# A mamba and spectral-filter kernel: other order of the first loads, later constants, and a second block whose first tiles lie under tiles that are dead in the last chunk

## The chip, the cores and the metric

The kernel runs on one core of a Trainium2 chip. The metric is the device time of one execution in microseconds (us), the median of several runs. A core has five engines with a queue of instructions each: TensorE (PE, matmuls), VectorE (DVE), ScalarE (ACT), GpSimd (POOL) and SyncE (SP, which here only issues transfers). They meet through semaphores: an instruction that isn't ready holds all that stand behind it on its engine. Transfers (DMAs) run on 16 DMA engines that all queues share.

## The reference

Two layers in float32 on x of shape (4, 128, 128, 128): 4 images of 128 channels, with 128 x 128 = 16384 pixels that the first layer takes as a sequence.

```python
# layer 0, per image; l runs over 16384 pixels
h1 = relu(xf @ mlp_w1.T + mlp_b1);  xm = h1 @ mlp_w2.T + mlp_b2
x_in, z = split(xm @ in_proj_w.T)                 # 256 channels each
u = silu(causal_conv4(x_in) + conv_b)
dt, Bm, Cm = split(u @ x_proj_w.T)                # 8, 16, 16
delta = softplus(dt @ dt_proj_w.T + dt_proj_b)
h = h * exp(delta * A) + delta * B * u            # a scan over l, 256 x 16 states
y = sum_s(h * C) + u * D
out = (y * silu(z)) @ out_proj_w.T                # 128 channels
x1 = silu(group_norm(out, 4)) + x
# layer 1
a = relu(agg_w @ group_norm(concat(x1, x1), 32) + agg_b)
weights = softmax(mean(a) @ wg_w.T + wg_b)        # 4 per image
xf = rfft2(x1)
ff = rfft2(irfft2(xf * filter_f))                 # f = 0..3
result = irfft2(sum_f weights_f * xf * ff_f) + residual_weight * x1
```

## The kernel before, in words

**Block 0** takes the sequence of each image in 32 chunks of 512 pixels, so 128 chunks in all, k = 0 to 127. A chunk has 8 units (two halves j of the 256 channels, four groups r of four states), each of two pairs, so NP = 16 slots per chunk. A table `todo[slot, phase]` holds functions; a loop runs over the slots and, in each, over the phases ("turn", "sums", "pe", "exps", "late", "act", "pool", "dbu", "early", "gate", "scans", "dve", "end"), and calls them. This order, written by hand, is the order in which each engine's queue is filled (`tc.manual_schedule()`). `pre(k)` lists a chunk's preparation with slots counted from the chunk before: load of x, the small matrix products, the convolution (`cv_mm` into two of the "pp" banks of PSUM, `silu_act` out of them), x_proj (`xd_mm`, `xd_act`), dt (`dt_act` makes delta), and the product delta x u (`du_pool`, on POOL, L319).

The scan needs each channel's row on the partitions of several states. So delta, du, B and C are written to DRAM (dd, bc) and read back, repeated over partitions: `bc_load` reads rB and rC (L270, four transfers each), `rep_load(j)` reads rdelta and rdu (L327, four each). All are issued by SP, in order. A transfer that reads dd or bc waits for the store to have landed.

In a unit, ACT makes da = exp(delta A) (L400), POOL makes hb = rdu x rB for three of four states (L370, `dbu`), PE turns bt into b0 for the fourth (L390), DVE scans (L419) and multiplies two of the scans by rC (L421), POOL multiplies the others (L426), and PE sums over states (L440). PSUM has one bank each for b0, da1, da2 and da3, so ACT can't be far ahead of DVE.

`first_constants` loads what a chunk needs. `later_constants`, called in phase "end" of slot 4, loads out_wT (wo) and 15 constants of the norms and of block 1 on SP, then lets DVE negate fwm (L129) and set eps and ones (L131, L133). `later_products`, slot 8, has DVE make weff0 (L138, L139) and bias0 (L144), the latter from two matmuls of PE into a "pp" bank (L143).

From slot 26 on of each chunk, `post(k)` gates y with silu(z), multiplies by wo, takes sums for the norm (L463, L464) and stores o to DRAM (L465, on SP). The norms, the `agg` step of block 1 and some forward spectra of finished images run in the same slots, for images 0 to 2.

**Block 1** works in units of 8 channels of one image (64 units), three sub-blocks each: forward transform on PE (over_h, over_w; L873, L892; or a spectrum that block 0 stored, sx), the mix of the four filters by the image's weights (`term` on ACT L840, `mix` on POOL L850 or DVE L848), the products on DVE, the inverse transform, the residual (L949) and the store. The norm of image 3 runs among the first units. A filter tile ft has four transfers (L819) of 8 channels for one of the four filters each. SP loads, in order: the three constants c_ihc, c_ihs, c_iw (L764), xt1 and sx of the first unit, xt1 of the second, ft_0, and so on.

Tiles come from pools. A pool's memory is laid out once, and block 1's pools start at the address at which block 0's did, so that its tiles lie over block 0's. The first transfer into such a tile waits until the last reader or writer of what lies under it is done. Before, `late` and the big tiles of block 1 lie over p1 and p2 of block 0, which hold, among much else, small tiles that the softmax of image 2 uses to the end of block 0.

```python
        todo[4, "end"].append(partial(s.later_constants, s))
        todo[8, "end"].append(partial(s.later_products, s, psum))
```

Of the kernel before, what the change touches and what calls it, by code (L numbers as in the profile page):

```python
# [46 lines left out]
def kernel(ctx: ExitStack, tc: tile.TileContext, a: dict, out: bass.AP):  # L47
# [32 lines left out]
    def first_constants(s):  # L80
# [26 lines left out]
        for j in range(NH):  # L107
            nc.vector.tensor_scalar_mul(s.diag[:, j, :], s.ident, dvec[:, j : j + 1])

    def later_constants(s):  # L110
        s.wo = const("wo", [P, NH, C], a["out_wT"].rearrange("(j p) c -> p j c", p=P))
# [16 lines left out]
        s.fwm = const("fwm", [W, 2 * WF], a["c_fwi"])  # L128
        nc.vector.tensor_scalar_mul(s.fwm, s.fwm, -1.0)  # L129
        s.eps = cpool.tile([P, 1], F32, tag="eps", name="eps")  # L130
        nc.vector.memset(s.eps, EPS)  # L131
        s.ones = cpool.tile([P, P], F32, tag="ones", name="ones")
        nc.vector.memset(s.ones, 1.0)  # L133

    def later_products(s, psum):

        weff0 = s.weff0 = cpool.tile([P, C], F32, tag="weff0", name="weff0")
        nc.vector.tensor_scalar_mul(weff0, s.wagg[:, 0, :], s.gam[:, 0:1])  # L138
        nc.vector.scalar_tensor_tensor(weff0, s.wagg[:, 1, :], s.gam[:, 1:2], weff0, ALU.mult, ALU.add)  # L139
# [20 lines left out]
def block0(tc, s):  # L160
# [4 lines left out]
    with ExitStack() as ctx:  # L165
        def pool(name, bufs, **kw):
            return ctx.enter_context(tc.tile_pool(name=name, bufs=bufs, **kw))

        p1 = pool("p1", 1)
        p2 = pool("p2", 2)  # L170
        hpool = pool("hb", 4)
        tiny = pool("tiny", 2)
        dbc = pool("dbc", 2, space=DRAM)
        s.own, s.spare = p1, p2
        psp = pool("psp", 2, space=PSUM)
# [13 lines left out]
        def pre(k):  # L189
# [7 lines left out]
            def load():  # L197
                xt = d["xt"] = p1.tile([P, T], F32, tag="xt", name=f"xt_{k}")
                (nc.sync if k else nc.scalar).dma_start(out=xt, in_=s.xflat[b, :, i * T : (i + 1) * T])
# [6 lines left out]
            def h1_act():  # L206
                d["h1"] = p1.tile([P, NH, T], F32, tag="hd", name=f"h1_{k}")
                for j in range(NH):
                    nc.scalar.activation(d["h1"][:, j, :], ps["h", j], AF.Relu, bias=s.b1[:, j : j + 1])
# [47 lines left out]
            def xd_act():  # L257
                xd = d["xd"] = p1.tile([P, TH], F32, tag="xd", name=f"xd_{k}")
# [6 lines left out]
            def bc_load():  # L265
                for q, tag in enumerate("BC"):
                    t = d[tag] = p2.tile([P, NG - 1 + q, T], F32, tag=f"r{tag}", name=f"r{tag}_{k}")
                    rows = d["bc"][q, (1 - q) * SQ :, :].rearrange("(g s) t -> s g t", s=SQ)
                    for m in range(SQ):
                        nc.sync.dma_start(out=t[m * DG : (m + 1) * DG], in_=rows[m].partition_broadcast(DG))  # L270
# [8 lines left out]
            def dt_act():  # L279
                delta = d["delta"] = p1.tile([P, NH, T], F32, tag="hd", name=f"delta_{k}")  # L280
# [11 lines left out]
            def xd_turn_act():  # L292
                d["xdt"] = p1.tile([P, NT, NX], F32, tag="xdt", name=f"xdt_{k}")
                src = ps["xt"][:, 0:2, :].rearrange("p t (h r) -> p h t r", h=2)
                nc.scalar.copy(d["xdt"].rearrange("p (h t) r -> p h t r", h=2), src[:, :, :, 0:NX])
# [10 lines left out]
            def bt_act(h, n0, n1):  # L306

                if h == n0 == 0:
                    d["bt"] = p2.tile([P, NT, NH * ND, SQ, DG], F32, tag="bt", name=f"bt_{k}")
                for n in range(n0, n1):  # L310
# [6 lines left out]
            def du_pool():  # L317
                du = d["du"] = p1.tile([P, NH, T], F32, tag="du", name=f"du_{k}")
# [3 lines left out]
            def rep_load(j):  # L322
                for q, tag in enumerate(("delta", "du")):
                    t = d[tag, j] = p2.tile([P, ND, T], F32, tag=f"r{tag}", name=f"r{tag}_{k}_{j}")
                    rows = d["dd"][q, j * P : (j + 1) * P, :].rearrange("(g d) t -> d g t", d=DG)
                    for m in range(SQ):
                        nc.sync.dma_start(out=t[m * DG : (m + 1) * DG], in_=rows)  # L327
# [116 lines left out]
        def post(k):  # L444
# [12 lines left out]
            def o_act():  # L457
# [6 lines left out]
                nc.scalar.activation(d["po"], d["po"], AF.Square, accum_out=stats[b][:, 1, i : i + 1])  # L464
                nc.sync.dma_start(out=outs[b][:, i * T : (i + 1) * T], in_=d["o"])  # L465

# [271 lines left out]
def block1(tc, s):  # L738
# [10 lines left out]
    with ExitStack() as ctx:  # L749
        def pool(name, bufs, **kw):  # L750
            return ctx.enter_context(tc.tile_pool(name=name, bufs=bufs, **kw))

        late = pool("late", 1)
        p2 = pool("f2", 2)
        psa = pool("psa", 1, space=PSUM)
        psx = pool("psx", 2, space=PSUM)
# [5 lines left out]
        def const(name, shape):  # L762
            t = late.tile(shape, F32, tag=name, name=name)
            nc.sync.dma_start(out=t, in_=s.a[name])  # L764
            return t
# [32 lines left out]
        N = len(units)  # L798
        u = [SimpleNamespace() for _ in units]

# [15 lines left out]
        def load_filter(ft):  # L816
            ft.t = p2.tile([H, NF, CC, 2 * WF], F32, tag="ft", name=f"ft_{ft.first}", bufs=KEEP)
            for f in range(NF):
                nc.sync.dma_start(out=ft.t[:, f], in_=filt[:, f, ft.c0 : ft.c0 + CC, :])  # L819

        def load(n):
            if n < N:
                c0, b = units[n]
                u[n].xt = p2.tile([H, CC, W], F32, tag="xt1", name=f"xt1_{n}", bufs=6)
                nc.sync.dma_start(out=u[n].xt, in_=s.x1[b][c0 : c0 + CC].rearrange("c h w -> h c w"))
                u[n].early = units[n] in s.spectra
                if u[n].early:
                    u[n].sx = p2.tile([H, CC, 2, WF], F32, tag="sx", name=f"sx_{n}", bufs=2)
                    nc.sync.dma_start(out=u[n].sx, in_=s.spec[b][:, c0 : c0 + CC])
# [242 lines left out]
```

## Time and profile before

| | us |
|---|---|
| median of 3 runs (7092.60 to 7100.89) | 7099.01 |
| the profiled execution's own time | 7100.83 |
| its span, first to last instruction | 7099.1 |
| VectorE busy | 6843.7 |
| GpSimd busy | 6807.6 |
| ScalarE busy | 6144.4 |
| block 0 ends (last o computed) | 6391.7 |
| mean granted TensorE clock | 0.926 |

The profile is one execution. Busy time is the sum of an engine's instructions; a line of a timeline gives the start, the length, the engine, the line of the code, the operation, what it writes and reads, and in square brackets how long the engine had stood idle before it and what ended that. "x4" means four instructions merged into one line. An engine with q behind its name (SPq, ACTq) issues a transfer: the length is that of the issue, and the data moves later. Where an instruction waits for several things, the one that the profile names may not be the last.

### The profile page before, as it was taken

How to read it: one execution, taken by the hardware profiler on the slowest of the kernel's cores; microseconds unless marked ns; L12 is line 12 of the kernel's file. 1: busy time of each engine (PE TensorE's matmuls, PEld its weight loads, DVE VectorE, ACT ScalarE, POOL GpSimd, SP SyncE). 2: the span in 40 equal slices, each digit the busy share in tenths (PEclk: the TensorE clock that was granted, in tenths of full speed). 3: DMA queues.
4: the chain of work that ended last, by engine and by line, in shares of the span. 5: the costliest groups of instructions: out<-in, count | busy, mean ns of one | idle time of the engine just before them, and what ended most of it. 6: DMA issues, size and time to landing. Idle time of an engine off the chain costs nothing.

```text
span 7099.1 us, 95554 instructions
## 1 busy us (share of the span) xinstructions
PE 5656.9 (80%) x28724; PEld 2700.3 (38%) x28724; DVE 6843.7 (96%) x7901; ACT 6144.4 (87%) x13836; POOL 6807.6 (96%) x3010
## 2 busy tenths in 40 slices
PE   6777777787777778787787778887778787877999
PEld 2333333333333333333333333333333333327888
DVE  6999999999999999999999999999999999997877
ACT  6888888888888888888989888898988989878886
POOL 6999999999999999999999999999999999997887
PEclk8988898888989989999999999999999999989999
DMA  6667667667787767777777777777878777768865
GB/s 141 160 153 164 159 149 165 160 150 175 179 196 181 188 169 167 181 181 179 192 193 196 189 174 177 174 184 172 200 188 200 191 170 178 169 143 293 273 218 190
DMA packets 759513, 1288.54 MB, mean 182 GB/s; under 512 B 81728, under 2 KB 192848, under 8 KB 758992
## 3 DMA queue, kind: packets, MB, share of 16 engines
q1 hardware_dynamic: 758848, 1282.16, 72.5%
q8 instruction: 226, 3.70, 0.2%
q14 instruction: 295, 2.42, 0.1%
q10 hardware_dynamic: 144, 0.26, 0.0%
HBM read 1025.52 MB, written 256.58 MB: 181 GB/s over the span
## 4 chain that ended last, share of the span: by engine, by line
ACT 30%; DVE 24%; POOL 18%; PE 10%; issue 10%; DMA 7%; SPq 1%; DVEq 0%; ACTq 0%; POOLq 0%
DVE da L419 12%; ACT da L400 12%; POOL hb L370 10%; POOL hb L426 7%; DVE h L419 7%; ACT L400 3%; DVE hb L421 3%; DMA rdelta<-dd 2%; ACT bt L313 2%; PE px L892 2%; DMA rdu<-dd 2%; ACT L247 2%; ACT L283 1%; ACT delta L283 1%; PE y L440 1%
## 5 line engine op out<-in xcount | busy, mean ns | idle before, releaser
L370 POOL TENSOR_TENSOR hb<-rdu,rB 128x1536 f32<-128x1536 f32 (+2 forms) x1536 | 3612.4, 2370 | 41.6 <-DMA rdelta<-dd 21.2
L400 ACT ACTIVATE da<-rdelta,amat 128x512 f32<-128x512 f32 x4096 | 2792.3, 699 | 123.3 <-DVE h L419 119.3
L426 POOL TENSOR_TENSOR hb<-h,rC 128x1024 f32<-128x1024 f32 (+1 forms) x1048 | 2411.1, 2302 | 89.3 <-DVE h L419 76.6
L419 DVE TENSOR_TENSOR_SCAN da<-da,st,hb 128x512 f32<-128x512 f32 x2000 | 2449.3, 1268 | 38.0 <-ACT da L400 27.1
L421 DVE TENSOR_TENSOR hb<-da,rC 128x512 f32<-128x512 f32 x2064 | 1309.7, 673 | 2.2
L419 DVE TENSOR_TENSOR_SCAN h<-da,st,b 128x512 f32<-128x512 f32 x992 | 1258.7, 1269 | 1.9 <-PE b L390 1.9
L440 PE MATMUL y<-hb,sel 128*32 128x512 f32 x8192 | 1243.4, 681 | 2.9 <-POOL hb L426 2.7
L419 DVE TENSOR_TENSOR_SCAN h<-da,st,hb 128x512 f32<-128x512 f32 x976 | 1223.1, 1255 | 1.4 <-ACT da L400 1.4
L390 PE MATMUL b<-ident,bt 128*128 128x128 f32 x4096 | 723.7, 298 | 448.9 <-DVE h L419 325.2
L239 PE MATMUL pp_cv<-xm,wck 128*128 128x512 f32 x2048 | 1013.7, 640 | 1.5 <-ACT xm L222 0.8
L313 ACT ACTIVATE bt<-pt_dut,xdt 128x256 f32<-128x256 f32 x2048 | 837.6, 473 | 181.1 <-PE pt_dut L302 180.9
L390 PEld LDWEIGHTS b<-ident,bt 128*128 128x128 f32 x4096 | 524.6, 151 | 943.2 <-DVE h L419 650.7
L422 ACT COPY st<-da 128x1 f32<-128x1 f32 x2064 | 267.9, 160 | 441.3 <-DVE hb L421 437.0
L239 PEld LDWEIGHTS pp_cv<-xm,wck 128*128 128x128 f32 x2048 | 396.0, 204 | 651.7 <-issue 420.8
L302 PE MATMUL pt_dut<-ident,du 128*128 128x128 f32 x1024 | 207.8, 337 | 407.2 <-POOL du L319 391.4
L850 POOL TENSOR_TENSOR wb<-wb,term 128x1040 f32<-128x1040 f32 x166 | 398.8, 2403 | 62.0 <-ACT term L840 56.6
L436 PE MATMUL y<-u,diag 128*128 128x512 f32 x512 | 303.3, 676 | 183.7 <-DVE zs L450 181.8
L277 PE MATMUL pp_dt<-xd,wdt 128*128 128x256 f32 x1024 | 299.2, 418 | 149.9 <-ACT pp_o L464 141.2
L302 PEld LDWEIGHTS pt_dut<-ident,du 128*128 128x128 f32 x1024 | 132.2, 165 | 652.6 <-POOL du L319 528.5
L400 ACT ACT_TABLE_LOAD x262 | 336.1, 1283 | 12.2 <-DMA rdelta<-dd 7.6
L319 POOL TENSOR_TENSOR du<-delta,u 128x1024 f32<-128x1024 f32 x128 | 301.1, 2353 | 29.4 <-ACT delta L283 27.9
L228 PE MATMUL pp_z<-xm,win 128*128 128x512 f32 x512 | 275.6, 636 | 59.5 <-ACT fq L504 53.7
(167 smaller groups left out, 8209.6 us busy)
## 6 DMA issues: line engine op xcount, KB each, us to landing
rdelta<-dd SPq DMA_DIRECT2D x1024, 256.0 KB, 4.8
rdu<-dd SPq DMA_DIRECT2D x1024, 256.0 KB, 7.8
rC<-bc SPq DMA_DIRECT2D x512, 256.0 KB, 7.4
rB<-bc SPq DMA_DIRECT2D x512, 192.0 KB, 4.6
dd<-delta SPq DMA_DIRECT2D x256, 256.0 KB, 7.7
dd<-du SPq DMA_DIRECT2D x128, 512.0 KB, 6.6
ft<-in_filt_w SPq DMA_DIRECT2D x108, 520.0 KB, 6.7
ob<-o SPq DMA_DIRECT2D x128, 256.0 KB, 2.1
```

Source lines behind the costliest of these rows:

```text
L239: nc.tensor.matmul(ps["cv", j], w, d["xm"][:, t : t + T], start=t == 0, stop=t == KC - 1)
L302: nc.tensor.transpose(ps["dut"][:, 2 * t + j, :], d["du"][:, j, at : at + P], s.ident)
L313: nc.scalar.activation(d["bt"][:, 2 * h + t, :, q, :], src, AF.Copy, scale=d["xdt"][:, 2 * h + t, R + q : R + q + 1])
L370: nc.gpsimd.tensor_tensor(hb[:, p : p + n, :], d["du", j][:, m : m + n, :], d["B"][:, p - 1 : p - 1 + n, :], ALU.mult)
L390: nc.tensor.transpose(b[:, t * P : (t + 1) * P], src, s.ident)
L400: nc.scalar.activation(da, d["delta", j][:, m, :], AF.Exp, scale=s.amat[:, c : c + 1])
L419: nc.vector.tensor_tensor_scan(o, das[q], b, init, ALU.mult, ALU.add)
L421: nc.vector.tensor_tensor(hb[:, p + q, :], das[q], d["C"][:, p + q, :], ALU.mult)
L426: nc.gpsimd.tensor_tensor(hb[:, ps, :], h[:, q, :], d["C"][:, ps, :], ALU.mult)
L436: nc.tensor.matmul(y, s.diag[:, j, :], d["u"][:, j, :], start=True, stop=False)
L440: nc.tensor.matmul(y[m * DG : (m + 1) * DG, :], s.sel, d["hb", j, r][:, p, :], start=False, stop=r == NG - 1)
L850: nc.gpsimd.tensor_tensor(wb, wb, u[n].terms[f], ALU.add)
```

## The change

*First chunk.* For k = 0 alone, SP's loads come in the order rdelta, rB, (store of du), rdu, rC, and then the second half's; before it was rB, rC, (store of du), rdelta, rdu. Later chunks keep their order.

*Constants.* wo is loaded in slot 1 instead of 4. The other 15 are loaded in slot 17, behind the loads of chunk 1. The six DVE operations and the two matmuls of PE (fwm, eps, ones, weff0 twice, bias0) all stand in slot 33, behind the first unit of chunk 2.

*Pools.* A new pool pq at the start of block 0's memory takes tiles that are dead in the second half of the last chunk (wx, wdt, xt, h1 and delta, xd, xdt, du, and bt of even chunks); bt of odd chunks stays with the small tiles in p1. In block 1 the pool `ready`, at the same addresses, takes the three constants, the first of four ft, the first two of six xt1 and the first of two sx; the others stay in p2 with as many buffers less. The last o is stored by ACT's queue instead of SP's.

```diff
+    def output_weights(s):
+        s.wo = const("wo", [P, NH, C], ...)
     def later_constants(s):
-        s.wo = const("wo", [P, NH, C], ...)
...
-        nc.vector.tensor_scalar_mul(s.fwm, s.fwm, -1.0)
-        nc.vector.memset(s.eps, EPS)
-        nc.vector.memset(s.ones, 1.0)
     def later_products(s, psum):
+        nc.vector.tensor_scalar_mul(s.fwm, s.fwm, -1.0)
+        nc.vector.memset(s.eps, EPS)
+        nc.vector.memset(s.ones, 1.0)
...
+        pq = pool("pq", 1)
         p1 = pool("p1", 1)
...
-                d["bt"] = p2.tile([P, NT, NH * ND, SQ, DG], F32, tag="bt", name=f"bt_{k}")
+                home = p1 if k % 2 else pq
+                d["bt"] = home.tile([P, NT, NH * ND, SQ, DG], F32, tag="bt", name=f"bt_{k}")
...
-                (5 if k else 7, "act", bc_load), (6, "act", dt_act), (7, "act", xd_turn_act), (7, "pool", du_pool),
-                (8, "pe", partial(du_turn, 0)), (9, "act", partial(rep_load, 0)),
+                (5, "act", partial(bc_load, "BC" if k else "")), (6, "act", dt_act),
+                (6, "act", partial(rep_load, 0, () if k else ("delta",))), (6, "act", partial(bc_load, "" if k else "B")),
+                (9, "pe", partial(rep_load, 0, () if k else ("du",))), (9, "act", partial(bc_load, "" if k else "C")),
+                (7, "act", xd_turn_act), (7, "pool", du_pool),
+                (8, "pe", partial(du_turn, 0)), (9, "act", partial(rep_load, 0, ("delta", "du") if k else ())),
...
-                nc.sync.dma_start(out=outs[b][:, i * T : (i + 1) * T], in_=d["o"])
+                queue = nc.sync if k < B * NCH - 1 else nc.scalar
+                queue.dma_start(out=outs[b][:, i * T : (i + 1) * T], in_=d["o"])
...
-        todo[4, "end"].append(partial(s.later_constants, s))
-        todo[8, "end"].append(partial(s.later_products, s, psum))
+        todo[1, "end"].append(partial(s.output_weights, s))
+        todo[NP + 1, "end"].append(partial(s.later_constants, s))
+        todo[2 * NP + 1, "end"].append(partial(s.later_products, s, psum))
...
+        def home(n, first, bufs):
+            return (ready, {"bufs": 1}) if n < first else (p2, {"bufs": bufs - first})
...
-            ft.t = p2.tile([H, NF, CC, 2 * WF], F32, tag="ft", name=f"ft_{ft.first}", bufs=KEEP)
+            to, bufs = home(spans.index(ft) % KEEP, 1, KEEP)
+            ft.t = to.tile([H, NF, CC, 2 * WF], F32, tag="ft", name=f"ft_{ft.first}", **bufs)
...
-                u[n].xt = p2.tile([H, CC, W], F32, tag="xt1", name=f"xt1_{n}", bufs=6)
+                to, bufs = home(n % 6, 2, 6)
+                tag = f"xt1_{n % 6}" if to is ready else "xt1"
+                u[n].xt = to.tile([H, CC, W], F32, tag=tag, name=f"xt1_{n}", **bufs)
```

More of the change, by code (lines that the diff above doesn't have):

```diff
@@ L108, in first_constants @@
             nc.vector.tensor_scalar_mul(s.diag[:, j, :], s.ident, dvec[:, j : j + 1])
+    def output_weights(s):
+        s.wo = const("wo", [P, NH, C], a["out_wT"].rearrange("(j p) c -> p j c", p=P))
     def later_constants(s):
-        s.wo = const("wo", [P, NH, C], a["out_wT"].rearrange("(j p) c -> p j c", p=P))
         s.gnw = col("gn_w")
@@ L128, in later_constants, with later_products @@
         s.fwm = const("fwm", [W, 2 * WF], a["c_fwi"])
+        s.eps = cpool.tile([P, 1], F32, tag="eps", name="eps")
+        s.ones = cpool.tile([P, P], F32, tag="ones", name="ones")
+    def later_products(s, psum):
         nc.vector.tensor_scalar_mul(s.fwm, s.fwm, -1.0)
-        s.eps = cpool.tile([P, 1], F32, tag="eps", name="eps")
         nc.vector.memset(s.eps, EPS)
-        s.ones = cpool.tile([P, P], F32, tag="ones", name="ones")
         nc.vector.memset(s.ones, 1.0)
-    def later_products(s, psum):
         weff0 = s.weff0 = cpool.tile([P, C], F32, tag="weff0", name="weff0")
@@ L173, in block0 @@
         dbc = pool("dbc", 2, space=DRAM)
-        s.own, s.spare = p1, p2
+        s.own, s.spare = pq, p2
         psp = pool("psp", 2, space=PSUM)
@@ L197, in load @@
             def load():
-                xt = d["xt"] = p1.tile([P, T], F32, tag="xt", name=f"xt_{k}")
+                xt = d["xt"] = pq.tile([P, T], F32, tag="xt", name=f"xt_{k}")
                 (nc.sync if k else nc.scalar).dma_start(out=xt, in_=s.xflat[b, :, i * T : (i + 1) * T])
@@ L206, in h1_act @@
             def h1_act():
-                d["h1"] = p1.tile([P, NH, T], F32, tag="hd", name=f"h1_{k}")
+                d["h1"] = pq.tile([P, NH, T], F32, tag="hd", name=f"h1_{k}")
                 for j in range(NH):
@@ L257, in xd_act @@
             def xd_act():
-                xd = d["xd"] = p1.tile([P, TH], F32, tag="xd", name=f"xd_{k}")
+                xd = d["xd"] = pq.tile([P, TH], F32, tag="xd", name=f"xd_{k}")
                 nc.scalar.copy(xd, ps["xd"][:, 0:TH])
@@ L263, in xd_act, with bc_load @@
                     nc.sync.dma_start(out=rows[:, h * TH : (h + 1) * TH], in_=xd[h * HP + R : h * HP + NX])
-            def bc_load():
-                for q, tag in enumerate("BC"):
+            def bc_load(tags="BC"):
+                for tag in tags:
+                    q = "BC".index(tag)
                     t = d[tag] = p2.tile([P, NG - 1 + q, T], F32, tag=f"r{tag}", name=f"r{tag}_{k}")
@@ L279, in dt_act @@
             def dt_act():
-                delta = d["delta"] = p1.tile([P, NH, T], F32, tag="hd", name=f"delta_{k}")
+                delta = d["delta"] = pq.tile([P, NH, T], F32, tag="hd", name=f"delta_{k}")
                 d["dd"] = dbc.tile([2, DI, T], F32, tag="dd", name=f"dd_{k}")
@@ L292, in xd_turn_act @@
             def xd_turn_act():
-                d["xdt"] = p1.tile([P, NT, NX], F32, tag="xdt", name=f"xdt_{k}")
+                d["xdt"] = pq.tile([P, NT, NX], F32, tag="xdt", name=f"xdt_{k}")
                 src = ps["xt"][:, 0:2, :].rearrange("p t (h r) -> p h t r", h=2)
@@ L317, in du_pool, with rep_load @@
             def du_pool():
-                du = d["du"] = p1.tile([P, NH, T], F32, tag="du", name=f"du_{k}")
+                du = d["du"] = pq.tile([P, NH, T], F32, tag="du", name=f"du_{k}")
                 nc.gpsimd.tensor_tensor(du, d["delta"], d["u"], ALU.mult)
                 nc.sync.dma_start(out=d["dd"][1].rearrange("(j p) t -> p j t", p=P), in_=du)
-            def rep_load(j):
-                for q, tag in enumerate(("delta", "du")):
+            def rep_load(j, tags=("delta", "du")):
+                for tag in tags:
+                    q = ("delta", "du").index(tag)
                     t = d[tag, j] = p2.tile([P, ND, T], F32, tag=f"r{tag}", name=f"r{tag}_{k}_{j}")
@@ L751, in pool @@
             return ctx.enter_context(tc.tile_pool(name=name, bufs=bufs, **kw))
-        late = pool("late", 1)
+        ready = pool("ready", 1)
         p2 = pool("f2", 2)
+        def home(n, first, bufs):
+            return (ready, {"bufs": 1}) if n < first else (p2, {"bufs": bufs - first})
         psa = pool("psa", 1, space=PSUM)
@@ L762, in const @@
         def const(name, shape):
-            t = late.tile(shape, F32, tag=name, name=name)
+            t = ready.tile(shape, F32, tag=name, name=name)
             nc.sync.dma_start(out=t, in_=s.a[name])
@@ L798, in block1 @@
         N = len(units)
-        u = [SimpleNamespace() for _ in units]
+        u = [SimpleNamespace(early=x in s.spectra) for x in units]
         spans = []
@@ L823, in load @@
                 c0, b = units[n]
-                u[n].xt = p2.tile([H, CC, W], F32, tag="xt1", name=f"xt1_{n}", bufs=6)
+                to, bufs = home(n % 6, 2, 6)
+                tag = f"xt1_{n % 6}" if to is ready else "xt1"
+                u[n].xt = to.tile([H, CC, W], F32, tag=tag, name=f"xt1_{n}", **bufs)
                 nc.sync.dma_start(out=u[n].xt, in_=s.x1[b][c0 : c0 + CC].rearrange("c h w -> h c w"))
-                u[n].early = units[n] in s.spectra
                 if u[n].early:
-                    u[n].sx = p2.tile([H, CC, 2, WF], F32, tag="sx", name=f"sx_{n}", bufs=2)
+                    to, bufs = home(sum(e.early for e in u[:n]) % 2, 1, 2)
+                    u[n].sx = to.tile([H, CC, 2, WF], F32, tag="sx", name=f"sx_{n}", **bufs)
                     nc.sync.dma_start(out=u[n].sx, in_=s.spec[b][:, c0 : c0 + CC])
```

## The prediction

> **What bounds the kernel now.** I read the engine shares first, then busy time by stretch, then the timelines of the three places that the diff touches, and last the waits and the built order of both programs.
>
> ```profile
> PE 5656.9 (80%) x28724; PEld 2700.3 (38%) x28724; DVE 6843.7 (96%) x7901; ACT 6144.4 (87%) x13836; POOL 6807.6 (96%) x3010
> ```
>
> In block 0 DVE and POOL bound together: from 155 to 210 us DVE is busy 54.97 of 55 us and POOL 53.55; POOL starts each L426 product some 0.2 us after the DVE scan it needs. A microsecond that DVE loses there is lost for good, so what can be won lies where DVE stands still: the first 100 us and the change of blocks at 6391 us. The first chunk (timeline; columns start, length, engine):
>
> ```profile
> 28.72 1.83 SPq L270 DMA_DIRECT2D rB<-bc  x4
> 30.59 1.85 SPq L270 DMA_DIRECT2D rC<-bc  x4
> 33.30 3.92 SPq L327 DMA_DIRECT2D rdelta<-dd  x4
> 41.67 1.73 SPq L327 DMA_DIRECT2D rdu<-dd  x4
> 51.90 6.83 POOL L370 TENSOR_TENSOR hb<-rdu,rB 128x1536 f32<-128x1536 f32 x2 [21.23 <-DMA rdelta<-dd]
> 55.36 1.22 DVE L419 TENSOR_TENSOR_SCAN h<-da,hb 128x512 f32<-128x512 f32 x1 [3.68 <-POOL hb L370]
> ```
>
> The steady flow begins at 55.36, when POOL has rB and rdu. (The releaser named is rdelta; of what L370 reads, rdu comes last.) Then the constants:
>
> ```profile
> 77.43 0.43 SPq L72 DMA_DIRECT2D fwm<-in_c_fwi  x1
> 79.36 0.23 DVE L129 TENSOR_SCALAR fwm<-fwm 128x130 f32<-128x130 f32 x1 [11.12 <-DMA fwm<-in_c_fwi]
> 90.92 2.65 DVE L138 TENSOR_SCALAR weff<-wagg,gn_gamma 128x128 f32<-128x128 f32 x1
> 93.61 2.34 DVE L139 SCALAR_TENSOR_TENSOR weff<-wagg,gn_gamma,weff 128x128 f32<-128x128 f32 x1
> ```
>
> And the change of blocks:
>
> ```profile
> 6391.71 0.32 SPq L465 DMA_DIRECT2D ob<-o  x1
> 6393.03 0.30 ACT L713 ACTIVATE wts<-lg,total 128x4 f32<-128x4 f32 x1 [0.23 <-DVE total L710]
> 6393.35 0.33 SPq L764 DMA_DIRECT2D c_ihc<-in_c_ihc  x1
> 6396.34 2.50 SPq L819 DMA_DIRECT2D ft<-in_filt_w  x4
> 6403.70 1.16 ACT L840 ACTIVATE wb<-ft,wts 128x1040 f32<-128x1040 f32 x1 [10.38 <-DMA ft<-in_filt_w]
> 6406.05 12.13 POOL L850 TENSOR_TENSOR wb<-wb,term 128x1040 f32<-128x1040 f32 x5 [20.88 <-ACT term L840]
> ```
>
> SP stands in order behind the last store and behind L713, whose tiles lie under the new ones; ACT idles 10.38 us for the filter.
>
> **What the Trainium skill says.** "SBUF — State Buffer", Who interferes with whom: VectorE and GpSimd share one port pair, and an instruction that needs it blocks until the other's has ended. The trace agrees: L138 and L139, on 128 elements a partition, last 2.65 and 2.34 us and end with the POOL instructions that run beside them (93.49, 95.80), while fwm took 0.23 with POOL idle. "DMA: Bandwidth & Descriptors", Queues, rings and completion order: descriptors of one ring are taken in order. I use this as first in, first out; the trace agrees below. Same page, Issuing engines are not separate DMA queues: a store moved to ACT's queue saves issue time only. "ScalarE: Activation LUTs", What ACT_TABLE_LOAD costs: about 1283 ns; the trace has 1283.
>
> **The change, part by part.**
>
> *First chunk's loads.* Model: from 30.1 us (first bytes of rB, by the DMA rate in slices of 1.5 us) the DMA engines are full until 60.8 and move 6.55 MB, 214 GB/s. In order, rB (0.79 MB) 3.7 us, rC (1.05) 4.9, store of du (0.52) 2.4, rdelta 4.9, rdu 4.9 end at 33.8, 38.7, 41.1, 46.0, 50.9; rdu's issue at 41.67, the exps' table load at 46.78 and POOL at 51.90 fit, each 0.6 to 1.0 later. New order: rdelta, rB, store of du, rdu, rC. The first half of delta is stored at 27.70 and landed 2.1 us later (median of its issues), 29.8; first bytes 1.3 us on, 31.1; rdelta to 36.0, rB 39.7, store of du 42.1, landed 42.6. Only then may rdu be issued, and nothing stands behind it to fill the engines: a hole of 1.3 us, 43.9 to 48.8, POOL at 49.7. So **2.2 us** come off, not the 10 by which rdelta moves: ACT's early exps only wait for POOL's product. Bounds 0.5 (if stores land late) to 4. rC then ends at 53.7; its readers come at 49.7 + 6.83 = 56.5, hidden under POOL's two products by 2 us, and each us later than that would cost one.
>
> *Constants.* Before, 16 issues (0.48 us each) hold SP from 70.18 to 77.86, and DVE from 68.23 to 79.65 (wait, fwm, two memsets); da2 was ready by 68.45: **11.2 us** come off. L138, L139 and the bias hold DVE from 91.01 to 95.94: **4.9 us** off. wo moves ahead: one issue into an idle queue. The 15 others now follow rdu of chunk 1 (116.02 before) and take 15 x 0.48 = 7.2 us, ahead of xt of chunk 3 (117.92, needed some 25 us later) and of bc (133.23): they fit in 15 us of SP's idle time and cost nothing. Can the rest follow? POOL's idle time between 51.9 and 117 is 12.9 us, so POOL moves up 15.1 at most and DVE 18.3; L370 of chunk 2's first unit ends 4.2 us before its scan needs it (163.98 against 168.20), which covers the 3.2. rdu of chunk 1: bc at 67, then 5.0 MB at 214 GB/s, lands at 94; POOL gets to it at 96.
>
> *What is added.* The six DVE operations now stand after the first unit of chunk 2 (172.98 before). In the built order the two matmuls of bias0 wait for the silu of chunk 3, because both psp banks hold its convolution; DVE's bias0 waits for them, and every scan stands behind it.
>
> ```profile
> 172.91 1.27 DVE L419 TENSOR_TENSOR_SCAN h<-da,st,b 128x512 f32<-128x512 f32 x1
> 174.40 1.28 ACT L247 ACT_TABLE_LOAD   x1
> 176.66 1.25 ACT L244 ACTIVATE u<-pp_cv,conv_b 128x512 f32<-128x512 f32 x2
> ```
>
> Two exps, a table load, silu of z and the first u end at 177.3; the matmuls (0.85 us at 91.05, on a TensorE clock of 0.5) and bias0 (0.15): 178.2, so the scan of 172.91 is 5.3 us late. fwm, L138 and L139 meanwhile wait for the port. POOL, some 3 us behind by then, has L426 and two pieces of L370 left, to about 5.9 us; 6.6 at most if each of the memsets waits too. I take **6.0 lost** (bounds 5.0 and 9). It could cost less only where DVE is ahead of POOL, which the 3.2 above already use. Cadence: 0.5 for POOL's lag. Start: 2.2 + 11.2 + 4.9 - 6.0 - 0.5 = **11.8 us**, bounds 5 and 16.
>
> *Change of blocks.* SP now issues c_ihc to xt1_0 behind the store of chunk 126 (6353.38; x1 of the last agg between, issued 6361.72 as before and needed at 6381.43), then sx_0, xt1_1 and ft_0; 3.2 MB at some 380 GB/s (the rate from 6400 to 6420) land before 6375, under chunk 127's scans. The last store goes to ACT (about 0.4 us) behind L464, at 6392.2, and lands 2.1 us later (median of ob's stores), 6394.3; L713 ends at 6393.7. The first wb (L840, now L858) waits for both: 6394.4 against 6403.70, **9.3 us**, bounds 8 and 10. xt1_2 and ft_3 wait for the same, 4.5 us earlier than before and with seven transfers fewer ahead: 2.7 MB land by 6403, and only the fourth unit reads ft_3, after 6411. ACT, POOL, DVE and PE all start on that wb, so the shift goes through: DVE is 97% busy from 6440 to 6600, PE 97% from 6800.
>
> *At nothing:* bt in p1 or pq, and ft, xt1 and sx split over two pools, remain rings of 2, 4, 6 and 2; the built programs have the same waits in all other chunks and units. If a ring lost a slot, that would be late loads in each of the 16 channel groups.
>
> Sum: 11.8 + 9.3 = 21.1 us. On the profiled span 7099.1: 7078. The profiled run took 7100.83, within the runs shown (7092.60 to 7100.89, median 7099.01): the median too becomes 7078.
>
> **Rivals.** (1) *The stall of chunk 2 eats the start*: fwm, memsets and both L13x each wait for a whole POOL operation (about 2.4 us, 12 in all), and rC or rdu is late by 2: start +3, total 12, 7087. For it: L139 did wait for a second one. Against: POOL runs dry once DVE stands. (2) *The filter queue absorbs the blocks' gain*: DMA is 0.87 to 1.03 busy from 6460 to 6600. Then only the start is left, 7087. Against: the DMA share is 0.01 from 6430 to 6440, so loads wait for tiles there. (3) *Slower*: rdu and rB lie at other addresses; if L370 (1536 calls) ran 23 ns longer, the 35 us would eat the 21 gained and 14 more, 7113. Against: each form stays in a narrow band over the buffers it rotates through (3.42 to 3.52 us for 1536 elements), and hb and h don't move. (4) *The early loads don't start early*, because a tile beneath them lives on: 7087. Against: c_ihc's only wait in the built order is a transfer of 6345. (5) *More*: POOL has nothing left when fwm comes and rdu is at 48: 7071.
>
> **How the numbers follow.** Main case 66% (7074 to 7083), (5) 14%, (1) 8%, (2) 4%, (4) 3%, (3) 5%. 7066 to 7089 takes in the cases at 7071 and 7087 with a run spread of 2 either way, and leaves out (3) and the tails. A measurement can tell 0.2% (14 us) from no change: below 7085 is faster. Main case and (5): 0.80; (1), (2) and (4): 0.15 the same; slower 0.05.
>
> **What would show it.** Right: L370's first product near 49.7; no 11 us wait for fwm; a DVE gap of 5 to 7 us between 155 and 162 at bias0, which waits for PE; the scan after it some 12 us earlier than 172.91; the first wb 2 to 3 us after the last o, some 21 us earlier than 6403.70; later chunks 49 us apart as before. Wrong: DVE waiting for rC or L370 before 60 us, ACT waiting for ft after the change of blocks, or a cadence of chunks that has changed.

## The result, and the profile after

The changed kernel takes 7071.96 us (median of 6 runs, 7067.90 to 7073.20) against 7098.02 us for the kernel before beside it (6 runs, 7092.60 to 7102.64): ratio 0.9964, 95% interval 0.9954 to 0.9975. That is 26.1 us less, where 21 were forecast (7078, range 7066 to 7089). The profiled execution took 7072.05 us, its span is 7070.2 us, 28.9 less than the span before.

Line numbers are those of the changed kernel: L370, L419, L426 of before are now L379, L428, L435; L713, L840, L850 are L724, L858, L868. The busy times of DVE, ACT and POOL have hardly moved (DVE 6843.7 before), so the difference is time in which these engines stood still:

```profile
PE 5638.4 (80%) x28724; PEld 2692.3 (38%) x28724; DVE 6844.2 (97%) x7901; ACT 6146.8 (87%) x13836; POOL 6810.6 (96%) x3010
```

The first chunk, timeline of the kernel after (start, length, engine):

```profile
28.21 1.76 SPq L333 DMA_DIRECT2D rdelta<-dd  x4
30.07 1.79 SPq L274 DMA_DIRECT2D rB<-bc  x4
31.96 0.38 SPq L325 DMA_DIRECT2D dd<-du  x1
39.73 1.73 SPq L333 DMA_DIRECT2D rdu<-dd  x4
46.52 6.82 POOL L379 TENSOR_TENSOR hb<-rdu,rB 128x1536 f32<-128x1536 f32 x2 [17.39 <-DMA rdu<-dd]
49.99 1.22 DVE L428 TENSOR_TENSOR_SCAN h<-da,hb 128x512 f32<-128x512 f32 x1 [7.65 <-POOL hb L379]
```

rdu is issued 7.77 us behind the store of du, because it waits for that store to land; POOL starts at 46.52 instead of 51.90. Part of that is not the change's: softplus starts at 25.45 instead of 26.98, and no instruction ahead of it was changed. Counted from the start of softplus, rdu is issued only 0.4 us sooner than before (14.28 against 14.69). What is gone are the bytes of rdelta just ahead of it: from the issue of rdu to POOL's start it takes 6.8 us instead of 10.2. The 11-us wait for fwm at 79 us and the 5 us of L138 and L139 at 91 us are gone. In their place, in slot 33 (same view):

```profile
149.53 2.36 POOL L435 TENSOR_TENSOR hb<-h,rC 128x1024 f32<-128x1024 f32 x1
151.31 4.19 DVE L136 TENSOR_SCALAR fwm<-fwm 128x130 f32<-128x130 f32 x1
151.85 3.56 POOL L379 TENSOR_TENSOR hb<-rdu,rB 128x512 f32<-128x512 f32 x2
155.79 0.86 PE L145 MATMUL pp_bias<-gn_beta,wagg 128*128 128x1 f32 x4 [2.00 <-ACT u L247]
156.69 0.16 DVE L146 TENSOR_TENSOR bias<-pp_bias,agg_b 128x1 f32<-128x1 f32 x1 [0.57 <-PE pp_bias L145]
156.77 1.27 DVE L428 TENSOR_TENSOR_SCAN h<-da,st,b 128x512 f32<-128x512 f32 x1
```

DVE is out of the scans from 151.31 to 156.77: 5.46 us. Of these fwm takes 4.19 and ends just after POOL's L379 (155.41); bias0 then waits only another 0.57 for PE, which waits for the silu of chunk 3. The first 4.19 us would have read as an expensive multiplication if the kernel before had not shown the same one at 0.23.

The change of blocks (same view):

```profile
6336.14 0.43 SPq L779 DMA_DIRECT2D c_ihc<-in_c_ihc  x1
6342.82 2.13 SPq L835 DMA_DIRECT2D ft<-in_filt_w  x4
6372.95 0.60 ACT L472 ACTIVATE o<-pp_o 128x512 f32<-128x512 f32 x1 [4.07 <-PE pp_o L464]
6373.67 0.34 ACTq L475 DMA_DIRECT2D ob<-o  x1
6375.87 1.16 ACT L858 ACTIVATE wb<-ft,wts 128x1040 f32<-128x1040 f32 x1 [0.59 <-DMA ob<-o]
6378.22 12.13 POOL L868 TENSOR_TENSOR wb<-wb,term 128x1040 f32<-128x1040 f32 x5 [10.98 <-ACT term L858]
```

The filter is issued 30 us ahead of the last o, and the first wb comes 2.92 us after it (12.71 before). What it waits for is the landing of the last store of o.

### The profile page after: what moved, and what is told of

Same layout as the page of the kernel before. It is cut to its first block, busy times and chain, and to the rows that moved or that the text cites. A ratio compares the mean times of both kernels' runs of the same rounds, so it can differ in the third digit from the quotient of the medians.

```text
span 7070.2 us, 95562 instructions
## 1 busy us (share of the span) xinstructions
PE 5638.4 (80%) x28724; PEld 2692.3 (38%) x28724; DVE 6844.2 (97%) x7901; ACT 6146.8 (87%) x13836; POOL 6810.6 (96%) x3010
## 4 chain that ended last, share of the span: by engine, by line
ACT 34%; DVE 28%; PE 11%; issue 10%; POOL 10%; DMA 6%; SPq 1%; DVEq 0%; ACTq 0%; POOLq 0%
DVE da L428 14%; ACT da L409 14%; DVE h L428 8%; POOL hb L379 5%; POOL hb L435 4%; ACT L409 4%; DVE hb L430 4%; DMA rdelta<-dd 2%; ACT bt L318 2%; ACT L250 2%; ACT L287 2%; ACT delta L287 2%; PE y L449 2%; PE px L910 2%; ACT zs L250 1%
## 5 line engine op out<-in xcount | busy, mean ns | idle before, releaser
L379 POOL TENSOR_TENSOR hb<-rdu,rB 128x1536 f32<-128x1536 f32 (+2 forms) x1536 | 3617.5, 2374 | 34.1 <-DMA rdu<-dd 26.2
L435 POOL TENSOR_TENSOR hb<-h,rC 128x1024 f32<-128x1024 f32 (+1 forms) x1048 | 2415.8, 2306 | 77.8 <-DVE h L428 64.6
L428 DVE TENSOR_TENSOR_SCAN da<-da,st,hb 128x512 f32<-128x512 f32 x2000 | 2449.7, 1268 | 35.6 <-ACT da L409 27.3
L428 DVE TENSOR_TENSOR_SCAN h<-da,st,b 128x512 f32<-128x512 f32 x992 | 1259.0, 1269 | 2.0 <-PE b L399 1.9
L428 DVE TENSOR_TENSOR_SCAN h<-da,st,hb 128x512 f32<-128x512 f32 x976 | 1223.5, 1256 | 1.5 <-ACT da L409 1.4
L242 PE MATMUL pp_cv<-xm,wck 128*128 128x512 f32 x2048 | 1004.2, 635 | 1.4 <-ACT xm L225 0.8
L242 PEld LDWEIGHTS pp_cv<-xm,wck 128*128 128x128 f32 x2048 | 392.4, 202 | 641.3 <-issue 413.4
L868 POOL TENSOR_TENSOR wb<-wb,term 128x1040 f32<-128x1040 f32 x166 | 399.2, 2405 | 49.9 <-ACT term L858 44.0
```

Of the source, the lines that this page charges most:

```text
L242: nc.tensor.matmul(ps["cv", j], w, d["xm"][:, t : t + T], start=t == 0, stop=t == KC - 1)
L379: nc.gpsimd.tensor_tensor(hb[:, p : p + n, :], d["du", j][:, m : m + n, :], d["B"][:, p - 1 : p - 1 + n, :], ALU.mult)
L428: nc.vector.tensor_tensor_scan(o, das[q], b, init, ALU.mult, ALU.add)
L435: nc.gpsimd.tensor_tensor(hb[:, ps, :], h[:, q, :], d["C"][:, ps, :], ALU.mult)
L868: nc.gpsimd.tensor_tensor(wb, wb, u[n].terms[f], ALU.add)
```

## A common measure for all runs

The span of one execution can be cut at four events: the start of softplus of chunk 0 (nothing of the change is ahead of it), the o of chunk 4, the o of chunk 32, the last o (chunk 127), the end. In us, from one profiled execution of each kernel:

```
                         softplus   to o of 4   4 to 32   32 to 127   to the end
before                     26.98      301.81    1362.99    4699.21      708.11
after                      25.45      287.37    1362.99    4697.14      697.25
first order only           26.93      298.20    1363.06    4696.28      705.83
constants only             27.07      290.06    1363.06    4698.13      705.98
pools only                 27.97      301.81    1363.06    4697.33      694.53
after, last store on SP    27.09      286.99    1363.05    4697.60      697.27
products in slot 40        23.82      292.55    1362.97    4698.98      695.88
only bias0 in slot 33      26.05      287.55    1362.99    4697.11      697.30
all products early         25.32      281.89    1363.09    4700.51      695.89
rB and du first            26.96      285.20    1363.01    4702.12      697.91
both                       25.56      280.06    1363.09    4695.63      693.96
after, again               28.22      286.98    1362.98    4691.69      696.83
slot 40, weff0 first       28.35      292.39    1363.03    4695.64      697.59
slot 40, fwm by a column   28.93      292.43    1363.02    4703.35      694.87
```

The third column is the same for all within 0.12 us: chunks 4 to 32 go in lockstep, whatever came before. The first and the fourth vary by several us between executions, also between the two of the kernel after (2.8 and 5.5 us), so a part's effect is read from the second and the last column; the two of the kernel after agree there within 0.4. The last column still spreads over 4 us (693.96 to 697.91) among the eleven kernels with the new pools, whose block 1 is the same, so a single value of it is no finer than that. Of the 28.9 us between the two profiles, 1.5 are in the first column, 14.4 in the second, 2.1 in the fourth and 10.9 in the last.

## Experiments

### The three parts, each alone

The *first order*: the kernel before with only this.

```diff
-(5 if k else 7, "act", bc_load), (6, "act", dt_act),
+(5, "act", partial(bc_load, "BC" if k else "")), (6, "act", dt_act),
+(6, "act", partial(rep_load, 0, () if k else ("delta",))), (6, "act", partial(bc_load, "" if k else "B")),
+(9, "pe", partial(rep_load, 0, () if k else ("du",))), (9, "act", partial(bc_load, "" if k else "C")),
...
```

> The kernel before with only the new order of the first chunk's loads (rdelta, rB, store of du, rdu, rC in place of rB, rC, store of du, rdelta, rdu). Theory that the parts add up: POOL's first product starts about 20 us after softplus starts instead of 24.9 us after, so 2 to 5 us come off, less whatever the granted clock does before delta is ready; about 7094 in all, and the 11-us wait for fwm stays, shifted with the rest. The prediction's own size of this step: 2.2 us, 7096. Rival, that the early order only works together with the later constants: SP reaches the constants no earlier, fwm lands as before, and 0 us come off, 7098.

Measured: 7093.50 us, ratio 0.9994 (0.9985 to 1.0002); by the second column 3.6 us off. The time alone does not tell this from nothing, the trace does. Timeline of this kernel:

```profile
41.15 1.77 SPq L329 DMA_DIRECT2D rdu<-dd  x4
48.03 3.43 POOL L375 TENSOR_TENSOR hb<-rdu,rB 128x1536 f32<-128x1536 f32 x1 [17.41 <-DMA rdu<-dd]
75.57 0.23 DVE L129 TENSOR_SCALAR fwm<-fwm 128x130 f32<-128x130 f32 x1 [11.19 <-DMA fwm<-in_c_fwi]
```

With softplus at 26.93, POOL starts 21.1 us after it, as in the kernel after, and not 24.9 as before (24.2 in the two kernels below, which keep the old order). The wait for fwm is as long as ever and has come forward by 3.8 us: SP reaches the constants by way of the store of chunk 1's B and C, which moves with everything else. The rival (nothing gained without the later constants) falls.

The *constants* alone, with the two lines of the table:

```diff
-todo[4, "end"].append(partial(s.later_constants, s))
-todo[8, "end"].append(partial(s.later_products, s, psum))
+todo[1, "end"].append(partial(s.output_weights, s))
+todo[NP + 1, "end"].append(partial(s.later_constants, s))
+todo[2 * NP + 1, "end"].append(partial(s.later_products, s, psum))
```

> The kernel before with only the moves of wo, of the 15 other constants and of the products that use them (to the slots that the change gives them). Parts add up: the waits of 11.2 and 5.0 us in the first 100 us go, a stall of 5 to 6 us comes in the first unit of chunk 2, 10 to 11 us off: 7087 to 7088. Rival, that POOL (which had that time to catch up) becomes the bound: 5 us or less off, 7093 or more.

Measured: 7083.96 us, ratio 0.9982 (0.9975 to 0.9989); second column 11.75 off. POOL starts 24.15 us after softplus here, against 24.92 before; the next kernel has 24.25 and is no sooner at chunk 4 for it, so this difference can't simply be taken off the 11.75. DVE stands from 156.06 to 161.25, 5.2 us, in slot 33. The rival (5 us or less) falls.

The *pools* alone:

```diff
+pq = pool("pq", 1)
...
-s.own, s.spare = p1, p2
+s.own, s.spare = pq, p2
...
-late = pool("late", 1)
+ready = pool("ready", 1)
...
```

> The kernel before with only the moves of tiles between pools and the last store on ACT's queue. Parts add up: nothing moves before 6372 us, the first wb of block 1 comes 3 us after the last o instead of 12.7 us after: 9 to 10 us off, 7088 to 7089. Rival, that the moved tiles cost something in block 0 (other addresses, rings in two pools): the time from the first scan to the last o grows by more than 1 us.

Measured: 7086.61 us, ratio 0.9985 (0.9979 to 0.9992). The second and third columns are those of the kernel before (301.81 in both), so the moved tiles cost nothing there; the first wb comes 2.91 us after the last o (6393.08 and 6390.17). Together the three medians lie 3.7, 13.2 and 10.5 us below the kernel before, 27.4 against 26.1 for the whole; in the second column 3.6 + 11.75 against 14.4 (14.8 in the second profile of the kernel after). So the parts add up to within 1 us; on top of the constants the order is worth 2.7 to 3.1 (290.06 against 287.37 and 286.98), not 3.6.

### The last store's queue

```diff
-queue = nc.sync if k < B * NCH - 1 else nc.scalar
+queue = nc.sync
```

> The kernel after with the last store of o back on SP's queue, where it stands ahead of the loads of block 1. Theory that SP's order is what held the loads: the constants, x1, spectrum and filter loads of block 1 are issued only after that store, about 0.7 us after the last o; only the wait for the last softmax weights (1.3 us) is still saved, and 8 to 9 of the 9.8 us come back: 7080 to 7081. Rival, that it was the tiles under the loads that held them and the queue of the store makes no odds: first wb 3 us after the last o, 7072, as after.

Measured: 7072.16 us, ratio 0.9965 (0.9951 to 0.9978): the theory is wrong and the rival right. Timeline of this kernel:

```profile
6344.60 2.66 SPq L835 DMA_DIRECT2D ft<-in_filt_w  x4
6375.44 0.33 SPq L475 DMA_DIRECT2D ob<-o  x1
6377.63 1.16 ACT L858 ACTIVATE wb<-ft,wts 128x1040 f32<-128x1040 f32 x1 [0.57 <-DMA ob<-o]
```

In the built program the first loads of block 1 stand ahead of the last store on SP, although the code calls them after it. In the kernel before they stand behind it, but it isn't the store that holds them there: its issue is over at 6392.03, and c_ihc goes at 6393.35, when L713 has ended (6393.33), whose tiles lie beneath. The store is issued 0.7 us after o on either queue and lands as early. With the new pools the move of the store is worth nothing, and the tiles' addresses do it all; the move of the store without the new pools was not run.

### The stall of slot 33: port, PE, or both

Two waits lie in it: fwm's, which ends with POOL, and bias0's, for PE. The products in slot 40, where both "pp" banks are free and PE is not late:

```diff
-todo[2 * NP + 1, "end"].append(partial(s.later_products, s, psum))
+todo[2 * NP + 8, "end"].append(partial(s.later_products, s, psum))
```

> The kernel after with the six products 7 slots later (end of slot 40 in place of 33), where both psp banks are free: bias0's matmuls no longer wait for a silu, DVE still shares its port with POOL. Theory 1, as the prediction has it (PE's wait sets the length of the stall): the stall of 5.4 us falls to 1 to 1.5, about 4 us off, 7068. Theory 2 (the wait of fwm for the port sets it by itself): stall 4 to 5 us, at most 1 off, 7071. Theory 3 (the two waits lie side by side, either alone is enough): as theory 2.

Measured: 7077.69 us, ratio 0.9976 (0.9967 to 0.9985): 17.5 us off the kernel before instead of 26, and the second column is 5.2 us longer than in the kernel after. No theory had that. Timeline of this kernel:

```profile
169.94 3.45 POOL L379 TENSOR_TENSOR hb<-rdu,rB 128x1536 f32<-128x1536 f32 x1
170.35 8.95 DVE L136 TENSOR_SCALAR fwm<-fwm 128x130 f32<-128x130 f32 x1
170.96 0.85 PE L145 MATMUL pp_bias<-gn_beta,wagg 128*128 128x1 f32 x4
173.33 2.37 POOL L435 TENSOR_TENSOR hb<-h,rC 128x1024 f32<-128x1024 f32 x1
175.65 3.57 POOL L379 TENSOR_TENSOR hb<-rdu,rB 128x512 f32<-128x512 f32 x2
185.97 2.34 POOL L435 TENSOR_TENSOR hb<-h,rC 128x1024 f32<-128x1024 f32 x1 [6.76 <-DVE h L428]
```

PE has bias0 ready at 171.8, long before it is wanted. But fwm waits through four POOL instructions in a row (L379, L435 and two more of L379), to 179.22, when POOL has nothing left that doesn't need a new scan of DVE's. Then it is POOL that stands, 6.76 us, until DVE has made that scan. Against theory 1 this says that the port alone makes a stall; its length is POOL's backlog (8.9 us here, 4.1 in slot 33), not one instruction. DVE is out of the scans for 9.55 us (170.35 to 179.90), 4.1 more than in slot 33; a wait of 1.11 us at 193.50, which the kernel after doesn't have, makes up the 5.2.

Now the reverse: the port's users early (`later_products` without bias0) and bias0 alone in slot 33 (`later_bias`):

```diff
-todo[NP + 1, "end"].append(partial(s.later_constants, s))
-todo[2 * NP + 1, "end"].append(partial(s.later_products, s, psum))
+todo[min(n for n, _ in todo), "end"].append(partial(s.later_constants, s))
+todo[-8, "end"].append(partial(s.later_products, s, psum))
+todo[2 * NP + 1, "end"].append(partial(s.later_bias, s, psum))
...
+    def later_bias(s, psum):
...
```

> The kernel after with the 15 constants loaded right behind the first ones (from 9 us, SP idle) and fwm, the two memsets and both products of weff0 done by DVE in its idle time before 40 us; only bias0 (two matmuls and DVE's addition) stays in slot 33. No wait for the port is left there, PE's wait is. Theory 1: stall still 5.3 us, 7072. Theory 2: stall 0.2 to 1, about 5 us off, 7067. Theory 3: as theory 1. The earlier loads (0.7 MB while the DMA engines are nearly idle) should move nothing else; if delta's chain came later, all would shift.

Measured: 7070.16 us, ratio 0.9964 (0.9950 to 0.9978); second column 287.55 against 287.37. Timeline of this kernel:

```profile
17.74 0.23 DVE L136 TENSOR_SCALAR fwm<-fwm 128x130 f32<-128x130 f32 x1 [7.19 <-DMA fwm<-in_c_fwi]
157.54 0.16 DVE L149 TENSOR_TENSOR bias<-pp_bias,agg_b 128x1 f32<-128x1 f32 x1 [5.34 <-PE pp_bias L148]
```

The 4.19 us of fwm have become 0.23 in idle time, and nothing is won: bias0 waits 5.34 for PE. Theory 2 (the port by itself) falls. With bias0 early too, `later_products` whole in slot -8 (the difference to the kernel just above, whose split of the function goes as well):

```diff
-todo[2 * NP + 1, "end"].append(partial(s.later_bias, s, psum))
...
```

> As b2, with bias0 too done before 40 us: neither wait is left in slot 33. All three theories: the stall of 5.4 us is gone, 7066 to 7067. Rival: POOL, which caught up during the stall, becomes the one that DVE waits for, and 3 us or less come off, 7069 or more.

Measured: 7068.70 us, ratio 0.9963 (0.9948 to 0.9978); second column 5.5 us less than after, the whole stall. The rival (POOL becomes the bound) falls: chunks 4 to 32 go on in lockstep with 5.5 us kept. The times alone don't tell this kernel from the one above (7064.26 to 7070.94 against 7066.78 to 7072.84); the traces do. The three runs together speak for theory 3, two waits side by side: taking fwm's away alone won nothing, taking both away won all. The other half, fwm's wait alone in slot 33, was not run; from the trace of the kernel after it would leave some 4.8 us (an estimate: 151.31 to 156.11, the end of weff0's products there). In this execution 3.4 us were lost again after chunk 32 (fourth column), which the second run of the kernel after shows to be within what executions differ by.

### What decides how long the port is kept

In the kernel before, L138 and L139 waited for one POOL instruction each (2.65 and 2.34 us; 2.66 and 2.34 in the two kernels above that leave the products in slot 8, first order only and pools only), fwm here for four. Is that the form of the instruction? The kernel of slot 40 with weff0's two products first:

```diff
+nc.vector.tensor_scalar_mul(weff0, s.wagg[:, 0, :], s.gam[:, 0:1])
+nc.vector.scalar_tensor_tensor(weff0, s.wagg[:, 1, :], s.gam[:, 1:2], weff0, ALU.mult, ALU.add)
 nc.vector.tensor_scalar_mul(s.fwm, s.fwm, -1.0)
...
-nc.vector.tensor_scalar_mul(weff0, s.wagg[:, 0, :], s.gam[:, 0:1])
-nc.vector.scalar_tensor_tensor(weff0, s.wagg[:, 1, :], s.gam[:, 1:2], weff0, ALU.mult, ALU.add)
```

> The kernel of b1 (products in slot 40, POOL with some 9 us of work queued) with the two products of weff0 ahead of the negation of fwm and the memsets. Theory A (whatever comes first waits until POOL has nothing queued): weff0's first product takes 8 to 9 us, all others are short. Theory B (weff0's products get in at the end of one POOL instruction, as in the kernel before, 2.65 and 2.34 us; the negation of fwm does not, it waits for POOL to run dry): each product 2 to 3.5 us, the negation then takes the 2 to 4 us that POOL still has.

and the same kernel with fwm first, but multiplied by a column of -1:

```diff
+nc.vector.memset(s.minus, -1.0)
...
-nc.vector.tensor_scalar_mul(s.fwm, s.fwm, -1.0)
+nc.vector.tensor_scalar_mul(s.fwm, s.fwm, s.minus)
```

> The kernel of b1 with fwm multiplied by a column of -1 instead of the constant -1 (the form of weff0's first product, 130 elements a partition in place of 128, in place in the same tile). Theory A (POOL's queue decides): 9 us, as in b1. Theory B1 (the form of the scalar decides): 2 to 3.5 us. Theory B2 (the form of the scalar does not matter, the place in time or in memory does): 9 us.

One execution each, 7078.89 and 7084.45 us (kernel before beside them: 7102.08). Timeline of the first:

```profile
174.74 8.92 DVE L137 TENSOR_SCALAR weff<-wagg,gn_gamma 128x128 f32<-128x128 f32 x1
183.70 0.35 DVE L138 SCALAR_TENSOR_TENSOR weff<-wagg,gn_gamma,weff 128x128 f32<-128x128 f32 x1
183.97 0.22 DVE L139 TENSOR_SCALAR fwm<-fwm 128x130 f32<-128x130 f32 x1
```

and of the second:

```profile
175.33 8.97 DVE L138 TENSOR_SCALAR fwm<-fwm,minus 128x130 f32<-128x130 f32 x1
184.37 0.16 DVE L142 TENSOR_SCALAR weff<-wagg,gn_gamma 128x128 f32<-128x128 f32 x1
```

Whichever stands first waits 8.9 to 9.0 us, and all behind it are short: theory A for this place, the form doesn't matter. What let the pair in between two POOL instructions in slot 8 stays open. It is no accident of one execution, since three kernels show it alike, and POOL's queue there has the same instructions in the same order (du, L370, L426, two more of L370) as in slot 40.

### The hole ahead of rdu

DMA share (last but one column) and GB/s of the kernel after by stretch:

```profile
36.00:38.00 2.00, 1.84 (x7) 0.69 (x5) 0.00 (x0) 1.98 (x5) 0.00 (x0) 1.00 1.03 223
38.00:39.00 1.00, 0.00 (x0) 0.00 (x0) 0.00 (x0) 0.99 (x2) 0.00 (x0) 1.00 0.98 377
39.00:40.00 1.00, 0.00 (x0) 0.00 (x0) 0.00 (x0) 1.00 (x3) 0.00 (x0) 0.97 0.08 27
40.00:41.00 1.00, 0.39 (x1) 0.18 (x1) 0.00 (x0) 1.00 (x3) 0.00 (x0) 0.50 0.29 63
41.00:42.00 1.00, 0.38 (x2) 0.29 (x2) 0.88 (x1) 1.00 (x3) 0.00 (x0) 0.50 1.06 315
```

From 39 to 41 us the DMA engines do little (0.08 and 0.29): 1.6 us in which nothing is under way while rdu waits for du's store and is then started. With the order rB, store of du, rdelta, rdu, rC the 1.05 MB of rdelta come in between:

```diff
-(6, "act", partial(rep_load, 0, () if k else ("delta",))), (6, "act", partial(bc_load, "" if k else "B")),
+(6, "act", partial(bc_load, "" if k else "B")),
+(7, "act", xd_turn_act), (7, "pool", du_pool), (8, "turn", partial(rep_load, 0, () if k else ("delta",))),
...
-(7, "act", xd_turn_act), (7, "pool", du_pool),
```

> The kernel after with the first chunk's loads in the order rB, store of du, rdelta, rdu, rC: rdelta's 1.05 MB now fill the time in which rdu waits for the store of du to land. Theory (a hole of about 1.3 us before rdu, and the store of du queued behind rdelta): rdu is issued about 4 us earlier and lands 1.3 to 2.5 us earlier, POOL's first product starts about 18.5 to 19.7 us after softplus starts (21.1 in the kernel after), 7070. Rival (no hole; the DMA engines are busy throughout, the bytes ahead of rdu are the same): 0 us, 7072.

Measured: 7065.82 us, ratio 0.9962 (0.9947 to 0.9977); POOL starts 19.4 us after softplus instead of 21.1, second column 2.2 us less. Timeline of this kernel, and its DMA share:

```profile
30.66 0.38 SPq L325 DMA_DIRECT2D dd<-du  x1
31.09 3.28 SPq L333 DMA_DIRECT2D rdelta<-dd  x4
36.44 1.73 SPq L333 DMA_DIRECT2D rdu<-dd  x4
```

```profile
34.00:36.00 2.00, 1.93 (x8) 0.73 (x7) 0.00 (x0) 2.00 (x6) 0.00 (x0) 0.92 1.06 358
36.00:38.00 2.00, 2.00 (x6) 0.74 (x4) 0.00 (x0) 1.31 (x4) 0.00 (x0) 1.00 1.05 210
38.00:40.00 2.00, 1.63 (x6) 0.68 (x5) 0.00 (x0) 1.21 (x4) 0.00 (x0) 1.00 1.06 211
```

The store of du stands behind 0.79 MB instead of 1.84 (rdu is issued 5.8 us after it instead of 7.8), and from 34 to 40 us the share stays above 1. The rival (no hole) falls.

### Both improvements together

> The kernel after with both edits that took something off in its own trace: constants and all six products before 40 us, and the first chunk's loads in the order rB, store of du, rdelta, rdu, rC. Theory that they add: counted from the start of softplus, chunk 4 comes 5.5 + 2.2 = 7.7 us earlier than in the kernel after, 7064 in all. Rival, that POOL's lag becomes the bound once both waits are gone: 5.5 us or less, 7067. Either way faster than both kernels.

Beside it the kernel after, on the same chip:

> The kernel after, unchanged, beside the one above on the same chip, so that the two are compared under the same conditions: 7072, and in its trace the same 5.4-us stall in slot 33; the start of softplus and the chunks after the 32nd show how far two executions of one kernel differ (1 to 4 us expected from the granted clock and the norms).

Measured: 7061.35 us (7058.96 to 7064.43, ratio to before 0.9952, 0.9938 to 0.9966) against 7069.25 us (7068.62 to 7073.66, 0.9963): 7.9 us apart, and the two sets of runs don't meet. Second column 280.06 against 287.37 and 286.98, so 6.9 to 7.3 of the 7.7 us expected: the parts add, apart from some tenths. The executions of the kernel after differ by 5.5 us between chunks 32 and 127, more than the 4 expected.

## Why the prediction was right, step by step

*What bounds the kernel.* Right. The three places where DVE stood still are where the time came from, and a stall of DVE in chunk 2 was lost for good: the second column has it at chunk 4, and it is still there 28 chunks later.

*First chunk's loads: 2.2 us (0.5 to 4).* Right in mechanism and sign, too small: 3.6 at chunk 4 alone (2.7 to 3.1 on top of the constants), and POOL starts 3.85 us sooner in the kernel after, counted from softplus. The mis-sized term is the way from softplus to the landing of du's store, put at 15.6 us (42.6 - 26.98); it was 14.3 (39.73 - 25.45), and 14.2 alone. All bytes had been costed at 214 GB/s, the 0.52 MB of that store at 2.4 us. In the slice that ends with its landing the DMA engines move 377 GB/s, at which they take 1.4. By the order of the queue that slice is the store's, but the trace has no line that says so, and the slice in which rdu's loads begin (41 to 42 us) shows 315: that the store moves faster than the loads is likely, not shown. The hole was forecast at 1.3 us, seen at 1.6, and filling it was worth 2.2.

*Constants: 11.2 + 4.9 us.* Right: neither wait is left, and the 15 loads in slot 17 delayed nothing that DVE waited for, though they hold SP for 12.8 us (95.94 to 108.74) and not 7.2.

*What is added: 6.0 us (5 to 9).* Right in size (5.4) and place, and the length forecast for PE's part alone, 5.3, is what bias0 alone cost (5.34). The step has fwm and both products of weff0 wait for the port "meanwhile", until POOL's three instructions are done. But fwm alone waited through all three, and the products behind it took 0.16 and 0.35. It forecast that this covered part would be as long as PE's or longer (5.9); fwm's was 4.19. That POOL's backlog would set the price of a port-using instruction anywhere in the flow was not seen: the same products seven slots later cost 9.55 us.

*Cadence: 0.5.* It was some 0.1 by this sum (3.85 + 11.2 + 4.9 - 5.46 = 14.5 at the places, with the prediction's sizes for the two waits that went; 14.4 at chunk 4).

*Change of blocks: 9.3 us (8 to 10).* 9.8 to the first wb, 10.9 to the end of the profiled span; means of the last column are 706.6 for the three kernels without the new pools and 696.3 for the eleven with them, 10.3 apart. Two sub-steps failed. The store on ACT's queue has no share in it, and "SP stands in order behind the last store" was not what held the loads: with the store on SP they are ahead of it. And the store is issued at 0.7 us after o, during the Square, not behind it; so it lands, and wb starts, some 0.5 us earlier than the step had it. (A reading to correct: DVE is 96% busy from 6440 to 6600 us, not 97%.)

*At nothing.* Right: with the pools alone, the time to chunk 4 and on to 32 is unchanged. The rival of slower addresses did not come: POOL's product has a mean of 2371 ns there and 2374 in the kernel after, against 2370 before, where the rival needed 23 more.

*Sum.* 11.8 + 9.3 = 21.1 forecast, 14.4 + 9.8 to 10.9 found; the rest of the 28.9 between the profiles (1.5 ahead of softplus, 2.1 between chunks 32 and 127) is of the kind in which executions of one kernel differ. Apart from the constants, every term was put too low in gain or too high in loss, so no luck of errors that cancel is in the sum, and the time came out 6 us under the forecast and within its range. Rival 5 (7071) came nearest in time, and half for its reason: rdu was early, but POOL still had 4.1 us of work when fwm came.

## What to carry to other kernels

Before a small operation is put into a flow in which VectorE and GpSimd run neck and neck, ask what GpSimd has queued at that point: an operation that needs the shared port may pay for all of it, and it costs nothing where GpSimd is idle. A stall with two waits in it shows only the one that ended last; take each away alone, and both, before judging either, since here the one that was taken away alone was worth nothing and both together 5.5 us. For loads that depend on a store, put independent bytes between the store and the load; and when one part of a change is said to matter (here the queue of a store), undo it alone.

## What the runs showed of the hardware that was not expected

The Trainium skill, "SBUF — State Buffer", Who interferes with whom, says that whoever issues first gets the shared ports for the whole instruction and the other blocks. Here VectorE stayed blocked across four GpSimd instructions in a row (8.95, 8.92 and 8.97 us in three kernels, two forms of the operation), until GpSimd had nothing to run, and across three in slot 33 (4.08 to 4.19 us in five executions). It got in after a single one in slot 8, in the three kernels that have the products there; why is open.

Softplus of the first chunk starts at 23.82 to 28.93 us in executions whose work up to there is the same but for loads that nothing there reads and small VectorE operations in idle time. The matmuls ahead of it show where the time goes. Those of the convolution (L239, L242 after) follow one another either 0.85 or 0.43 us apart, and executions differ in when the one turns into the other: at 17.2 us in the kernel before (weight loads at 16.38, 17.23, 17.70, 18.14), at 18.4 to 19.1 with the pools alone, and ahead of the convolution's first matmul, at 13.92, in the kernel after. From the first relu (L209, L212 after) to softplus it is 17.94, 19.26 and 16.43 us, and the difference of the first and the last is the whole of the 1.5 us between before and after. The granted clock says the same of two of them, 0.54 from 10 to 16 us before and 1.00 after, but it also reads 1.00 with the pools alone, where the matmuls are still 0.85 us apart; their spacing is the better witness. What sets the moment is open. Nor is it settled why executions agree within 0.12 us from chunk 4 to 32 and then differ by up to 11.7 us (4691.69 to 4703.35), when the norms and the spectra run beside the scans.
